# Storing a derived weight later, reading normalized rows back later, and choosing between operand and weights by what is scarce, in a fused graph layer

## The chip, the cores and the metric

The kernel runs on one core of a Trainium2 chip. The core has five engines that run side by side: TensorE (PE in the profile; its weight loads are PEld), VectorE (DVE), ScalarE (ACT), GpSimd (POOL) and SyncE (SP). Transfers are issued from queues of SP, ACT and POOL and run on 16 DMA engines. The metric is the device time of one execution in microseconds (us), as a median over several.

## The reference

Input are 32 graphs `b`, each with 512 nodes of 256 features, and an adjacency mask of 512 x 512 for each. All is computed in float32. Cut to what matters:

```python
h      = relu(layernorm(x))                      # [32, 512, 256]
c      = relu(bn(conv1(h)))                      # 1x1 convolution along the nodes
x_conv = relu(bn(conv2(c)) + h)                  # 17 taps, 256 -> 256 channels
s      = h @ w_se.T + b_se                       # 3 features
A      = exp(-|s_n - s_m|^2) * mask              # [512, 512] for each graph
x_nmp  = A @ relu(h @ w_msg.T + b_msg)
gi     = concat(x_conv, x_nmp) @ w_ih.T + b_ih   # GRU cell
gh     = h @ w_hh.T + b_hh
r, z   = sigmoid(gi_r + gh_r), sigmoid(gi_z + gh_z)
out    = x + (1 - z) * tanh(gi_n + r * gh_n) + z * h
```

## The kernel before

**Work.** Graphs come in 8 groups of 4. Five streams of work are interleaved by hand, each a Python generator:

- `rows` and `begins`: normalize a graph, turn it so that features lie on partitions, write that to DRAM (`HD`), and later run conv1 on it. For graphs 0 to 7 the turning is done by TensorE (`norm_t`); for graphs 8 to 31 it is done by the function `begin`: GpSimd's queue stores the normalized tile to DRAM (`XD_`, L791), SP's queue reads it back in 32-column blocks (8 transfers of 64 KB, `blocks`, L771), VectorE transposes the blocks in place (L799), GpSimd's queue stores the result (L802), and the input of the graph two further on is fetched.
- `conv`: the 17-tap convolution in a short-convolution form. For each group there are 25 products `m = 25 g + n`. Product `m` needs an operand `X2[m]`, which VectorE makes by subtractions from conv1's output, and a weight tile `WS[m]` in one of three buffers. In the first group (`m` below 25) VectorE and ScalarE make each weight from the 17 taps (`weights_first`), and ScalarE's queue stores it to DRAM. From `m = 25` on it is read back (`weights_again`, L470).
- In the second group (`m` from 25 to 49) a third part of each weight, the sum of its two parts, is made by VectorE in `third_weight` and stored by GpSimd's queue; from the third group on it is read back with the rest.
- `graphs`: messages, the factors of the squared distance (VectorE; `augl`, `augr`), their transposes, four exponentials (`kernel_exp`: four thin matmuls into `ps_b` and three `ps_g` banks, then four activations), the mask (`masked`; for graphs 0 to 7 TensorE transposes the mask tile `m_sb` and VectorE multiplies; for later graphs VectorE transposes), and the gather `A @ msg`. Mask tiles have three buffers; each use asks for the tile three further on.
- `gates`: the GRU matmuls into `ps_acc` and what follows them, from product 24 on. Before it `late_pools` (L686) loads the gates' weights (`whh` 768 KB, `wih` 1536 KB), and the first residual tiles (`res`, 8 transfers of 64 KB) follow on SP's queue.

**Order.** The scheduler is the loop at L1102. It keeps a planned clock `now`, which each matmul advances by an estimate, and planned times at which VectorE and ScalarE come free (`dve.free`, `act.free`). A generator yields the planned time at which it may go on. Work recorded with `later(t, f)` is issued when `now` reaches `t`. So a planned time does not make a queue wait; it sets where an instruction stands in the order of its queue. Each queue and engine then runs its instructions in that order and waits for semaphores. `background` fills VectorE with normalization, operands, weights and sums; its line L1013 asks first for an operand, then for a weight, then for a sum:

```python
near = at_product + 2
if len(X2) < near and operand_some() or len(WS) < near and prepare_some() or sum_some():
    return True
```

PSUM banks: `ps_c` has two, `ps_b` one, `ps_acc` two, `ps_g` three.

Of the kernel before, what the change touches and what calls it, by code (L numbers as in the profile page):

```python
# [44 lines left out]
def kernel(  # L45
# [28 lines left out]
    nc = tc.nc  # L74
# [23 lines left out]
    now = 5.0  # L98
# [23 lines left out]
    dve, act = Engine(nc.vector, 0.12, 0.00108), Engine(nc.scalar, 0.16, 0.0009)  # L122
# [21 lines left out]
    def later(t, f):  # L144
        LATER.append((t, f))
        LATER.sort(key=lambda e: e[0])
# [18 lines left out]
    def load(b, xs=None):  # L165
        if b not in XS:
            fetch(b, xs)
        NORMS[b] = norm(b)
        NORM_AT[b] = max(now + 7.0, 50.0) if b >= G else ARRIVES[b]
# [139 lines left out]
    def norm_t(b, d):  # L309
        xn = XS[b]  # L310
        if d == 0:
            HT[b] = front.tile([P, ND, N], F32, name="hT", bufs=2)
        ps = bank()
        for c in range(NT):
            turn(ps[:, c * P : (c + 1) * P], xn[:, c, d * P : (d + 1) * P])
        act.activation(HT[b][:, d, :], ps, AF.Relu)
        if d == ND - 1:
            XS.pop(b)
            nc.gpsimd.dma_start(HD[b], HT[b])
# [83 lines left out]
    WD = [dram.tile([P, 3, ND, D], F32, name=f"wd{n}") for n in range(25)]  # L403
# [17 lines left out]
    WS, W_AT = [], []  # L421
# [54 lines left out]
    def third_weight(m):  # L476
        if m in thirds:
            return
        thirds.add(m)
        w = WS[m]  # L480
        dve.tensor_tensor(w[:, 2], w[:, 0], w[:, 1], op=ALU.add)
        nc.gpsimd.dma_start(WD[m % 25][:, 2], w[:, 2])
        W_AT[m] = dve.free + LAG

    SUMS = []
# [96 lines left out]
    X2, X_AT, XD = [], [], {}  # L582
# [9 lines left out]
    def operand_some():  # L592

        nonlocal freed
        if len(X2) >= min(at_product + 1 + AHEAD, 25 * NG) or len(X2) >= 25 * made:
            return False
        if len(X2) == 25 * (made - 1) and now < made_at:
            return False
        got = next(xs)
        if got is not None:  # L600
            X2.append(got)
            X_AT.append(dve.free + LAG)
            if len(X2) % 25 == 21:
                freed = len(X2) // 25
        return True
# [3 lines left out]
    def prepare_some():  # L609
        nonlocal prepare_at  # L610
        if len(WS) >= 25 or len(WS) >= at_product + 3 or now < prepare_at:
            return False
        prepare_at = next(prepare)
        return True

    def convolution():
# [18 lines left out]
        for g in range(NG):  # L635
# [3 lines left out]
            for n in range(25):  # L639
# [8 lines left out]
                if 25 <= m + 1 < 50 and W_AT[m + 1] <= now:  # L648
                    third_weight(m + 1)
# [5 lines left out]
                if 25 <= m < 50:  # L655
                    third_weight(m)
                    yield W_AT[m]
# [110 lines left out]
    def blocks(t, rows, o):  # L768
        for g in range(P // 32):
            at = o * P + 32 * g  # L770
            nc.sync.dma_start(  # L771
                t[32 * g : 32 * g + 32, :].rearrange("i (k j) -> i k j", j=32),
                rows[:, :, at : at + 32],
            )
# [8 lines left out]
    def begin(b):  # L783

        nonlocal begun
        if b >= TURNED:
            yield lambda: b not in NORMS
            xs = XS.pop(b)  # L790
            nc.gpsimd.dma_start(XD_[b].rearrange("(c p) d -> p c d", p=P), xs)  # L791
            yield now + 4.5
            xb = xs.rearrange("p c d -> p (c d)").rearrange("p (o n) -> p o n", o=ND)
            for o in range(ND):
                blocks(xb[:, o, :], XD_[b].rearrange("(k i) d -> i k d", i=32), o)
            yield now + 8.0
            HT[b] = front.tile([P, ND, N], F32, name="hT", bufs=2)
            for o in range(ND):
                dve.transpose(HT[b][:, o, :], xb[:, o, :])  # L799
                if o < ND - 1:  # L800
                    yield dve.free
            nc.gpsimd.dma_start(HD[b], HT[b])  # L802
            begun = b + 1
            if b + 2 < B:
                load(b + 2)
            return
        if b == 2:
            yield lambda: told > 0
        yield lambda: b not in NORMS
        yield NORM_AT[b]  # L810
        for d in range(ND):
            norm_t(b, d)
            if d == ND - 1:
                begun = b + 1
                if b < 2 or b >= G:
                    load(b + (G if b < 2 else 2))
            yield now
# [177 lines left out]
    def sum_some():  # L995
        if not SUMS:
            return False
        SUMS.pop(0)()
        return True

    def norm_ahead(early=0.45):
        for b in list(NORMS)[:2]:
            if (b < G or clock["conv"] >= (b - G) / G - early) and norm_some(b):
                return True
        return False

    def background():

        nonlocal turn_of
        if norm_ahead(0.25):  # L1010
            return True
        near = at_product + 2
        if len(X2) < near and operand_some() or len(WS) < near and prepare_some() or sum_some():  # L1013
            return True
        for _ in range(3):
            turn_of += 1
            if (operand_some, norm_ahead, prepare_some)[turn_of % 3]():
                return True
        return False

    def fill():
        while LATER and LATER[0][0] <= now:
            LATER.pop(0)[1]()
        if EVAC:
            evacuate()
        while dve.free < now + 1.5 and background():
            pass
# [5 lines left out]
    def all_begins():  # L1033
        for b in range(G, B):
            yield lambda: b in XS and not rows_wait
            yield from begin(b)
# [3 lines left out]
    def all_rows():  # L1040
        nonlocal rows_wait
        for b in range(B):
            if b < G:
                yield from begin(b)
                yield act.free + LAG
            else:
                yield lambda: freed >= b // G - 1 and begun > b
                rows_wait = True
                load_row(b)
                yield now + 8.0  # L1050
            yield from rows(b)
            rows_wait = False
# [121 lines left out]
```

## Time and profile before

| | us |
|---|---|
| median of 4 runs | 2154.92 (2154.06 to 2155.49) |
| the profiled execution | 2154.06 |
| its span, first to last instruction | 2152.3 |
| TensorE busy in the span | 2095.5 (97%) |
| VectorE busy | 1523.1 (71%) |
| ScalarE busy | 762.1 (35%) |
| DMA read and written | 282.74 MB and 82.58 MB |

The span is what the engines' instructions cover; some 1.8 us of the execution lie around it. A busy share is an average over stages: the first 165 us make the weights of the first group, around 205 to 235 us the gates' weights are loaded, the last 150 us have only gates. Where TensorE is busy nearly all the time, what counts is when it is idle, on what it then waits, and at which clock it runs: PEclk is the granted share of the full clock, and a stage at 0.5 takes twice as long for the same matmuls. A wait is put down to the instruction whose semaphore came last.

### The profile page before, as it was taken

What the parts mean: (1) busy time and instruction counts of PE and PEld (TensorE: products, weight loads), DVE (VectorE), ACT (ScalarE), POOL (GpSimd) and SP (SyncE); (2) the same over time, 40 slices, a digit from 0 to 9 for tenths busy, and PEclk for the clock granted to TensorE, in tenths of its full rate; (3) what the DMA queues carried; (4) which work ended last, traced back from release to release, by engine and by line L of the source; (5) the groups of instructions that cost most, each with busy time, mean ns of one, the idle gap of its engine ahead of it and who ended that gap; (6) DMA issues with size and microseconds to landing.
All of it is one profiled execution on the core that took longest, in us unless ns stands there. A gap on an engine that the chain in (4) does not pass through costs nothing.

```text
span 2152.3 us, 26543 instructions
## 1 busy us (share of the span) xinstructions
PE 2095.5 (97%) x9200; PEld 1299.2 (60%) x9200; DVE 1523.1 (71%) x2818; ACT 762.1 (35%) x1277; POOL 296.2 (14%) x445
## 2 busy tenths in 40 slices
PE   7999799999999999999999999999999999999998
PEld 4877575566665666656665666656666566665443
DVE  6896788677776777667885777767777677776333
ACT  5545332433233342234324153243522324222311
POOL 2100112111111111111111111110111010011111
PEclk9999899999999999999999999999999999999999
DMA  7436667757676667765776766756675565554331
GB/s 271 171 133 224 207 208 199 203 158 192 150 225 163 176 177 200 201 191 144 204 189 183 207 151 187 196 168 189 180 193 150 152 162 144 148 160 92 69 74 35
DMA packets 539462, 367.12 MB, mean 171 GB/s; under 512 B 455232, under 2 KB 472000, under 8 KB 538688
## 3 DMA queue, kind: packets, MB, share of 16 engines
q1 hardware_dynamic: 511392, 282.95, 48.9%
q0 software_dynamic: 23248, 69.23, 10.1%
q10 hardware_dynamic: 4688, 13.24, 1.6%
q8 instruction: 73, 1.20, 0.2%
q14 instruction: 61, 0.50, 0.1%
HBM read 282.74 MB, written 82.58 MB: 170 GB/s over the span
## 4 chain that ended last, share of the span: by engine, by line
PE 95%; DVE 2%; ACT 1%; SPq 1%; DMA 0%; issue 0%; POOL 0%; ACTq 0%; DVEq 0%; POOLq 0%
PE ps_acc L127 46%; PE ps_g L127 20%; PE ps_c L127 19%; PE ps_b L127 7%; PE ps_g L132 2%; PE ps_b L733 1%; SPq L771 1%; ACT at L118 0%; ACT xconv L118 0%; DMA m_sb<-in_adj_dram 0%; DVE xconv L118 0%; DVE x L118 0%; PE ps_g L733 0%; ACT x_sb L118 0%; DMA x_sb<-in_x_dram 0%
## 5 line engine op out<-in xcount | busy, mean ns | idle before, releaser
L127 PE MATMUL ps_acc<-xconv,wih 128*128 128x512 f32 (+1 forms) x772 | 362.8, 592 | 6.0 <-ACT xconv L118 5.9
L127 PE MATMUL ps_acc<-xnb,wih 128*128 128x512 f32 (+1 forms) x772 | 362.6, 592 | 0.0
L127 PE MATMUL ps_acc<-hTb,whh 128*128 128x512 f32 x768 | 357.3, 595 | 0.0
L127 PE MATMUL ps_c<-xd,w 128*128 128x116 f32 x2800 | 343.0, 276 | 0.0
L127 PEld LDWEIGHTS ps_c<-xd,w 128*128 128x128 f32 x2800 | 329.3, 193 | 3.3 <-issue 3.1
L922 POOL DMA_DIRECT2D out_dram<-res x252 | 164.7, 660 | 976.4 <-DVE res L118 873.1
L118 DVE TENSOR_TENSOR r<-ps_acc,r 128x512 f32<-128x512 f32 (+1 forms) x65 | 44.4, 684 | 315.8 <-PE ps_acc L127 315.8
L127 PEld LDWEIGHTS ps_acc<-xnb,wih 128*128 128x128 f32 x772 | 141.6, 189 | 162.3 <-issue 160.4
L127 PEld LDWEIGHTS ps_acc<-xconv,wih 128*128 128x128 f32 x772 | 141.7, 190 | 159.6 <-issue 147.3
L127 PEld LDWEIGHTS ps_acc<-hTb,whh 128*128 128x128 f32 x768 | 142.1, 191 | 149.4 <-issue 145.4
L127 PE MATMUL ps_g<-at,msg 128*128 128x512 f32 x512 | 226.7, 593 | 0.9 <-DVE at L118 0.9
L127 PEld LDWEIGHTS ps_b<-x,w 128*128 128x128 f32 x1400 | 183.1, 192 | 69.8 <-issue 54.9
L118 ACT ACTIVATE mid<-ps_b 128x232 f32<-128x232 f32 x175 | 63.9, 365 | 369.3 <-PE ps_b L127 333.4
L127 PE MATMUL ps_b<-x,w 128*128 128x116 f32 x1400 | 184.6, 275 | 4.7 <-ACT at L118 4.7
L127 PEld LDWEIGHTS ps_g<-at,msg 128*128 128x128 f32 x512 | 96.1, 190 | 115.9 <-issue 111.4
L118 DVE SCALAR_TENSOR_TENSOR x<-x,x 128x480 f32<-128x480 f32 (+1 forms) x184 | 143.9, 782 | 2.8
L118 DVE TENSOR_TENSOR x<-x 128x240 f32<-128x240 f32 (+1 forms) x320 | 135.2, 462 | 0.6
L127 PE MATMUL ps_g<-wmsg,hTg 128*128 128x259 f32 x496 | 124.7, 382 | 0.7 <-ACT hT L118 0.7
L127 PE MATMUL ps_g<-hT,w 128*128 128x512 f32 x256 | 120.1, 613 | 2.3 <-ACT at L118 2.3
L127 PEld LDWEIGHTS ps_g<-wmsg,hTg 128*128 128x128 f32 x496 | 92.5, 190 | 45.1 <-issue 33.5
L118 DVE TENSOR_TENSOR xd<-x 128x480 f32<-128x480 f32 x175 | 113.5, 649 | 8.7 <-PE ps_c L127 8.7
L118 ACT ACTIVATE z<-ps_acc,brz 128x512 f32<-128x512 f32 x64 | 44.0, 687 | 208.6 <-PE ps_acc L127 208.4
(109 smaller groups left out, 2485.0 us busy)
## 6 DMA issues: line engine op xcount, KB each, us to landing
w<-wd SPq DMA_DIRECT2D x150, 768.0 KB, 5.9
m_sb<-in_adj_dram SPq DMA_DIRECT2D x384, 64.0 KB, 2.6
hd<-hT POOLq DMA_DIRECT2D x32, 512.0 KB, 6.0
res<-in_x_dram SPq DMA_DIRECT2D x256, 64.0 KB, 4.3
hTb<-hd SPq DMA_DIRECT2D x32, 512.0 KB, 6.2
xnb<-nd SPq DMA_DIRECT2D x64, 256.0 KB, 3.2
out_dram<-res POOLq DMA_DIRECT2D x252, 64.0 KB, 3.2
hTg<-hd SPq DMA_DIRECT2D x31, 512.0 KB, 4.4
```

Source lines behind the costliest of these rows:

```text
L118: getattr(self.engine, name)(*tiles, **more)
L127: nc.tensor.matmul(ps, lhsT, rhs, **more)
L132: nc.tensor.transpose(ps, a, ident)
L733: nc.tensor.matmul(pss[c], gr.left[k, :], gr.right[k, :], start=True, stop=True, tile_position=(32 * c, 0),)
L771: nc.sync.dma_start(t[32 * g : 32 * g + 32, :].rearrange("i (k j) -> i k j", j=32), rows[:, :, at : at + 32],)
L922: queue.dma_start(OB[b][:, s.start // 32 : s.stop // 32, o * P + 32 * g : o * P + 32 * g + 32], y[at, s].rearrange("i (k j) -> i k j", j=32),)
```

## The change

Three edits. In `third_weight` the store of the third part is recorded with `later` at VectorE's planned end plus 0.4, instead of at once; it stays on GpSimd's queue and there are 25 of it. In `begin` the planned time between the store of the normalized tile and its reading back goes from 4.5 to 7.0, for graphs 8 to 31. In `background` the two lists are sorted by length, and the shorter one is served first; at equal length the weights come first, where the operand did. All three alter where instructions stand in the queues; none adds or removes an instruction.

```diff
@@ third_weight
         dve.tensor_tensor(w[:, 2], w[:, 0], w[:, 1], op=ALU.add)
-        nc.gpsimd.dma_start(WD[m % 25][:, 2], w[:, 2])
+        later(dve.free + 0.4, lambda: nc.gpsimd.dma_start(WD[m % 25][:, 2], w[:, 2]))
         W_AT[m] = dve.free + LAG
@@ begin
             nc.gpsimd.dma_start(XD_[b].rearrange("(c p) d -> p c d", p=P), xs)
-            yield now + 4.5
+            yield now + 7.0
             xb = xs.rearrange("p c d -> p (c d)").rearrange("p (o n) -> p o n", o=ND)
@@ background
         near = at_product + 2
-        if len(X2) < near and operand_some() or len(WS) < near and prepare_some() or sum_some():
+        first = [(len(WS), prepare_some), (len(X2), operand_some)]
+        for n, some in sorted(first, key=lambda e: e[0]):
+            if n < near and some():
+                return True
+        if sum_some():
             return True
```

## The prediction

> **What bounds the kernel now.** I read the totals of the page first, then TensorE's waits, then busy time and clock by stretch, then SP's queue where the longest wait lies.
>
> ```profile
> span 2152.3 us, 26543 instructions
> PE 2095.5 (97%) x9200; PEld 1299.2 (60%) x9200; DVE 1523.1 (71%) x2818; ACT 762.1 (35%) x1277; POOL 296.2 (14%) x445
> ```
>
> TensorE is the bound. The changed program has the same matmuls in another order, so time can only come from its 57 us of idleness and from stretches at a lower clock. Its waits, over the whole span (who waits, for whom, total us, times, longest):
>
> ```profile
> PE ps_g L132 <- DMA m_sb<-in_adj_dram: 13.1, 1, 13.1
> PE ps_g L132 <- ACT x_sb L118: 9.3, 1, 9.3
> PE ps_acc L127 <- ACT xconv L118: 5.9, 5, 1.4
> PE ps_b L127 <- ACT at L118: 4.7, 5, 1.6
> PE ps_c L127 <- ACT w L118: 3.5, 2, 3.2
> PE ps_g L132 <- DVE augl L118: 2.4, 1, 2.4
> ```
>
> The 9.3 is the start and 5.2 of the xconv row lie in the last 150 us; both keep their order. The rest is within reach: one wait for a mask tile at 215.6 us, and many small ones between 60 and 150 us. Busy time by stretch (us, then PE, PEld, DVE, ACT, POOL with counts, then PEclk, DMA share, GB/s):
>
> ```profile
> 100.00:165.00 65.00, 59.73 (x417) 52.64 (x416) 57.09 (x101) 27.10 (x51) 4.30 (x5) 0.90 0.45 163
> 133.50:140.70 7.20, 3.49 (x17) 2.31 (x21) 7.03 (x17) 2.61 (x5) 0.54 (x1) 0.98 0.62 222
> 140.70:150.90 10.20, 8.69 (x43) 7.18 (x35) 8.11 (x21) 5.95 (x11) 1.31 (x1) 0.51 0.48 180
> 219.20:232.80 13.60, 4.11 (x8) 2.26 (x9) 8.07 (x15) 8.18 (x8) 1.10 (x2) 0.51 0.90 204
> 235.00:350.00 115.00, 114.28 (x590) 77.41 (x589) 95.25 (x190) 38.86 (x65) 22.61 (x35) 1.00 0.67 209
> 350.00:2000.00 1650.00, 1643.85 (x7119) 1007.30 (x7118) 1201.96 (x2190) 572.44 (x947) 223.90 (x329) 1.00 0.64 174
> ```
>
> The dearest lull apart from the mask is 133.5 to 150.9: TensorE idle for 3.71 + 1.51 us, then at half clock, which costs 8.69 x 0.49 = 4.3; together 9.5. VectorE is 88% busy from 100 to 165, so it is the next bound there. From 235 to 2000 TensorE loses under 7 us. SP's queue around the mask wait (start, us):
>
> ```profile
> 203.67 1.72 SPq L470 DMA_DIRECT2D w<-wd  x2
> 205.49 0.37 SPq L692 DMA_DIRECT2D whh<-in_w_hh_dram  x1
> 205.91 0.53 SPq L693 DMA_DIRECT2D wih<-in_w_ih_dram  x1
> 206.54 0.55 SPq L470 DMA_DIRECT2D w<-wd  x1
> 207.15 13.88 SPq L771 DMA_DIRECT2D res<-in_x_dram  x8
> 222.60 1.47 SPq L262 DMA_DIRECT2D m_sb<-in_adj_dram  x2
> ```
>
> The mask stands behind the gates' weights and eight `res` pieces: 24.9 us pass from the first `w` here to its landing (228.6), while TensorE arrives after 11.9.
>
> **The change, part by part.** Numbers are us, minus is faster. "New order" is the order in which the changed program's instructions stand on each engine and queue; durations are from the rows before.
>
> Edit 3, first effect, at 62 to 66 us: the fourth weight. TensorE waits 3.17 for ScalarE's `w`. Before, four `x_sb` activations (2.06) run ahead of it, in the new order two, so it comes 1.0 earlier. The half-clock stretch behind it (65.6 to 69.0) stays. A: **-1.0**, between -3.2 (whole wait) and 0 (the input for `w` is late too).
>
> Edit 3, second effect, graph 2's exponentials (134 to 151). Before, VectorE has two 1536-wide weight additions (1.75 + 1.76) between the second and third message; now there is one 1440-wide operand step (1.65). In front of the first message the new order has 0.8 more. So `augl` comes about 1.1 to 2.1 earlier, and 0.3 to 1.3 of the 2.38 wait is left; I take 0.9. The wait of 0.69 for `right` stays. The next two (1.14 for the exponentials, 0.38 for `w`) go: a whole product (32 records, 3.56) now stands between exponentials and mask, with its weight made before. Left are 1.6 idle and one half-clock stretch like that at 65.6 (3.4 x 0.47 = 1.6), 3.2 in place of 9.5. B: **-6.3**, between -9.5 and 0.
>
> What is late next is VectorE. In the new order graph 1's last mask is followed by its gather with no product between, so the multiplication (0.68) and what is queued before it is exposed; and two operands of the later products are made only shortly before TensorE comes to them, since it comes earlier. VectorE has 65 - 57.09 = 7.9 idle from 100 to 165, and 12.9 of 40 from 165 to 205, so most of A and B can be kept, not all. C: **+2.0**, between 0 (its idle time covers it) and +6.3 (all of B given back).
>
> The loading stage (203 to 233). Before, `hT` of graph 7 is ahead of the gates' weights on SP, which stood there until 203.26 (5.8 of it put down to a store). In the new order it is behind them, so loading can start when product 23 ends, 4.8 of TensorE's work earlier; the mask is needed 3.5 earlier. The mask still stands behind `w`, `whh`, `wih`, `w`, `res`, `hTb`, two `xnb`, and now that `hT` (512 KB); a store of `xd` (512 KB) leaves the stretch in exchange. From product 23's end TensorE has 2 x 1.78 of product, 1.1 of exponentials, 3.45 of conv1, 1.3 of transposes and a 1.15 wait for `at` until that mask: 10.6, against 11.9 before, so the wait itself grows by about 1.3 while its start comes 1.3 sooner. After the mask the gather now follows at once and waits for VectorE's multiplication, about 1.0, where gate matmuls stood; but one extra stop of SP is gone. D: **0**, between -15 (13.1 and the half clock behind it, 4.11 x 0.49) and +7.3 (one more block like the longest `res` issue).
>
> Exponentials followed directly by a product in `ps_b`, which has one bank: before this happens five times after 600 us, and each is a wait in the fourth row of the waits (0.67 to 1.62, mean 0.93; two are followed by 3.3 at clock 0.53, 1.55 lost each). By the new order there are six: two new (graph 4, and one near 1610 us), one gone (near 1300). E: **+1.5** = 0.93 + 3.1 / 5, between 0 and +3.2.
>
> Edit 1: 25 stores of 0.55 on GpSimd's queue. Before, 16 of them waited there, 110.5 in total, with `nd`, `xd`, `hd` and `out` stores behind; now these go first. The reload of a third part comes 25 products later, over 100 us, and the next weight load into the same buffer waits for a store that lands in 3.6. No TensorE wait hangs on either: **0**; if the cover goes, the five waits of weight loads on such stores (15.2 on SP) are the size, 0 to +3.
>
> Edit 2: 24 readbacks, each 8 issues (4.3 to 6.6 on SP), moved 2.5 later and thereby behind one or two weight, mask, `res` or fetch issues. SP waits 108.2 in 15 of them; at most 15 x 2.5 of it goes. What hides it: after 235 us TensorE has no wait on a DMA at all. VectorE's transposes, the `hd` store and the fetch of the graph two further on move too; conv1 needs them a group later. **0**, between -1.5 (a half-clock stretch less) and +3 (two more like 1427 us, 1.6 each).
>
> Sum: -1.0 - 6.3 + 2.0 + 0 + 1.5 = **-3.8**. Against the profiled execution's 2154.06 that is 2150.3; the median shown is 0.86 higher, so 2151.1.
>
> One rule bears on B and E. Rows first: 1.04 idle at 736.2 is followed by a stretch at 0.53; waits of 0.67 are not. The Trainium skill, page "TensorE: Matmul & The Clock Gate", section "HAM oscillation", asks only that TensorE have no idle gap over about 3.4 us. By that, waits of 1 to 3 us cost themselves alone; B would be -3.6, E +0.9, and the sum -1.7 (2153.2). The rows decide, and short waits are dearer than the rule says.
>
> **Rivals.** (1) The mask wait shrinks. For it: loading starts earlier by TensorE's work, and `xd` competes less. Against: as many bytes stand ahead of the mask, DMA share 0.9 to 1. With half of 13.1 and of the 2.0 of half clock behind it gone: 2151.1 - 7.6 = 2143.5. (2) Gains and new waits cancel, since VectorE sets the pace up to 205: C takes all of A and B, leaving E and its like: 2155 to 2157. (3) Slower: VectorE falls behind and each of three places where TensorE now waits for an operand or a mask product costs 2 to 3 and sets off a half-clock stretch of 1.6: 3 x (2.5 + 1.6) + 1.5 - 7.3 = +6.5, so 2161. It decides once those waits exceed about 1 us, the size that set off the clock before. For it: 88% busy. Against: 7.9 idle there. That the change does little of what it says is part of (2): SP's waits for `xd` are mostly longer than 2.5.
>
> **How the numbers follow.** My sum 0.42 (own range 2147 to 2154), rival 1 0.16, rival 2 0.14, rival 3 0.28. A measurement tells about 0.2% (4.3 us) from no change, so the line is at 2150.6: half of my case and rival 1 are faster (0.38), the other half and most of rival 2 within (0.32), the rest slower (0.30). The range 2140 to 2165 leaves out a fully vanished mask wait and more than rival 3.
>
> **What would show it.** A: the `w` wait near 62 us about 2. B: no stretch at half clock of 10 us near 140, `augl` wait under 1.3. C: new waits of `ps_c` or `ps_g` on DVE before 205, in sum near 2; over 5 speaks for rivals 2 or 3. D: one `m_sb` wait of 11 to 15; under 7 is rival 1. E: six `ps_b` waits. Edits 1 and 2: no TensorE wait on a DMA after 240; SP's `xd` wait under 108.2. I am wrong if a wait on a DMA appears after 240, or if the clock shows many more low stretches before 205.

## The result, and the profile after

The changed kernel takes 2160.54 us (median of 31 executions, 2157.54 to 2164.78), the kernel before 2155.26 (51 executions, 2152.12 to 2160.19). The ratio is 1.0022, with a 95% interval of 1.0017 to 1.0027: it is slower, by 5.3 us. The forecast was 2151.1, a gain. The time lies inside the stated range and where rival 3 put it (2161), but neither at the places that rival 3 named nor for its reason.

The profiled execution of the changed kernel took 2162.24, 1.7 above its median; that of the kernel before 2154.06, 1.2 below its own. So the two traces differ by 8.2, the medians by 5.3. The totals of the page after:

```profile
span 2160.1 us, 26532 instructions
PE 2096.2 (97%) x9200; PEld 1300.4 (60%) x9200; DVE 1523.5 (71%) x2818; ACT 763.6 (35%) x1277; POOL 296.8 (14%) x445
```

TensorE's busy time is the same within 0.7, its idle time went from 56.8 (2152.3 - 2095.5) to 63.9. So 7.1 of the 7.8 us that the span grew by is waiting; the mean granted clock is 0.989 in both profiles, since new stretches at half clock after 235 us replace longer ones before. TensorE's waits after (who waits, for whom, total us, times, longest):

```profile
PE ps_g L132 <- DMA m_sb<-in_adj_dram: 14.5, 1, 14.5
...
PE ps_b L127 <- ACT at L118: 5.3, 6, 1.6
PE ps_acc L127 <- ACT xconv L118: 5.2, 4, 1.3
PE ps_c L127 <- DVE z L118: 4.3, 2, 2.2
PE ps_c L127 <- DVE x L118: 2.7, 1, 2.7
PE ps_g L127 <- DVE at L118: 2.5, 3, 0.9
PE ps_c L127 <- ACT w L118: 2.2, 1, 2.2
PE ps_c L127 <- DVE sq L118: 1.9, 1, 1.9
PE ps_g L132 <- DVE augl L118: 1.2, 1, 1.2
```

Against before, `w` lost 1.3, `augl` 1.2, and three waits on ScalarE some 2.7 together. New are `z` (4.3, two waits), `x` (2.7) and `sq` (1.9), all of `ps_c` on VectorE; `m_sb` grew by 1.4, `at` on VectorE by 1.6, the `ps_b` row by 0.6. Busy time by stretch (us, then PE, PEld, DVE, ACT, POOL with counts, then PEclk, DMA share, GB/s):

```profile
235.00:350.00 115.00, 110.07 (x555) 75.91 (x554) 94.03 (x182) 40.11 (x65) 19.60 (x31) 0.97 0.62 184
350.00:2000.00 1650.00, 1643.82 (x7136) 1008.62 (x7135) 1203.97 (x2205) 571.09 (x949) 226.01 (x332) 1.00 0.64 176
```

The row to look at is 235 to 350. Before, TensorE was busy for 114.28 of it at a clock of 1.00; now for 110.07 at 0.97. From 350 to 2000 the two agree within 0.03. So the loss lies where the prediction had reckoned with next to none (under 7 us from 235 to 2000, in the order of before).

The SP queue around the mask, after, is the counterpart of the queue that the prediction shows of before. The weights, the eight residual pieces and the mask behind them are still in that order, and the mask tiles are asked at 216.65, while TensorE had been waiting since 208.6:

```profile
200.14 0.42 SPq L692 DMA_DIRECT2D whh<-in_w_hh_dram  x1
200.61 0.51 SPq L693 DMA_DIRECT2D wih<-in_w_ih_dram  x1
203.12 0.33 SPq L470 DMA_DIRECT2D w<-wd  x1
203.50 11.10 SPq L771 DMA_DIRECT2D res<-in_x_dram  x8
...
216.65 7.89 SPq L262 DMA_DIRECT2D m_sb<-in_adj_dram  x4
```

**The two new waits.** TensorE from 292 to 301 us (start, duration, engine, line, operation, count, and in brackets the idle time before it and its releaser):

```profile
292.01 1.04 PE L127 MATMUL ps_b<-x,w 128*128 128x116 f32 x8
292.89 1.95 PE L127 MATMUL ps_c<-xd,w 128*128 128x116 f32 x16
294.68 1.06 PE L127 MATMUL ps_b<-x,w 128*128 128x116 f32 x8
297.94 3.31 PE L127 MATMUL ps_c<-xd,w 128*128 128x116 f32 x16 [2.20 <-DVE z L118]
```

Two products follow each other. The second one's `ps_c` needs a bank that VectorE has not emptied yet. ScalarE and VectorE meanwhile:

```profile
290.50 0.60 ACT L118 ACTIVATE at<-ps_g 128x512 f32<-128x512 f32 x1 [2.84 <-PE ps_g L127]
292.21 0.69 ACT L118 ACTIVATE r<-ps_acc,brz 128x512 f32<-128x512 f32 x1 [1.12 <-PE ps_acc L127]
293.10 0.36 ACT L118 ACTIVATE mid<-ps_b 128x232 f32<-128x232 f32 x1 [0.19 <-PE ps_b L127]
293.36 3.86 ACT L118 ACTIVATE y<-z 128x1392 f32<-128x1392 f32 x3
...
297.25 0.64 DVE L118 TENSOR_TENSOR z<-ps_c,mid 128x464 f32<-128x464 f32 x1 [6.15 <-ACT y L118]
```

VectorE is idle for 6.15 us. It is to write the next `z`, which has one buffer, and ScalarE still has to read the old `z` three times (`y<-z`). The old `z` was complete at 288.9; the copies stand in ScalarE's queue behind three steps that wait for TensorE, so they start at 293.36. The kernel before has the same three copies at 277.25, where no product runs from 273.5 to 284.5:

```profile
277.25 3.86 ACT L118 ACTIVATE y<-z 128x1392 f32<-128x1392 f32 x3
```

Each fifth product starts a new `z`; here that place fell on two products in a row.

The second wait, at 332.60, is also for `z`, which starts at 331.92 there, and has another reason: `sum_all` (L487), which runs before a new `z`, ends with `settle`, which issues everything that was recorded for later. There that was the end of graph 0's gates:

```profile
326.86 1.61 DVE L118 TENSOR_TENSOR y<-y,z 128x1392 f32<-128x1392 f32 x1
328.39 0.68 DVE L118 TENSOR_TENSOR o_sb<-hTb,r 128x512 f32<-128x512 f32 x1
...
331.31 0.69 DVE L118 TENSOR_TENSOR res<-o_sb,res 128x512 f32<-128x512 f32 x1
331.92 1.18 DVE L118 TENSOR_TENSOR z<-ps_c,mid 128x464 f32<-128x464 f32 x2
...
332.60 3.66 PE L127 MATMUL ps_c<-xd,w 128*128 128x116 f32 x16 [2.06 <-DVE z L118]
```

Behind the first wait 16 matmuls take 3.31, behind the second 3.66, where 1.95 is usual: a stretch at half clock follows each (granted clock 0.58 from 297.9 to 301.3, 0.54 from 332.6 to 336.3). Together that is 2.20 + 1.36 + 2.06 + 1.71 = 7.3. The first stretch runs on into the next four matmuls (1.47 at 301.04, where 1.05 is usual), some 0.4 more.

### The profile page after: what moved, and what is told of

Read it like the earlier page. It is cut to its first block, busy times and chain, and to the rows that moved or that the text cites. A ratio compares the mean times of both kernels' runs of the same rounds, so it can differ in the third digit from the quotient of the medians.

```text
span 2160.1 us, 26532 instructions
## 1 busy us (share of the span) xinstructions
PE 2096.2 (97%) x9200; PEld 1300.4 (60%) x9200; DVE 1523.5 (71%) x2818; ACT 763.6 (35%) x1277; POOL 296.8 (14%) x445
## 4 chain that ended last, share of the span: by engine, by line
PE 83%; ACT 1%; DVE 1%; issue 0%; DVEq 0%; ACTq 0%
PE ps_acc L127 44%; PE ps_g L127 17%; PE ps_c L127 14%; PE ps_b L127 7%; PE ps_b L733 1%; PE ps_g L132 1%; ACT at L118 0%; DVE xconv L118 0%; ACT xconv L118 0%; ACT L118 0%; DVE r L118 0%; DVE o_sb L118 0%; PE ps_g L733 0%; DVE msg L118 0%; DVE res L118 0%
## 5 line engine op out<-in xcount | busy, mean ns | idle before, releaser
L118 ACT ACTIVATE mid<-ps_b 128x232 f32<-128x232 f32 x175 | 63.9, 365 | 370.7 <-PE ps_b L127 335.1
```

Source lines behind the costliest of these rows:

```text
L118: getattr(self.engine, name)(*tiles, **more)
```

## The experiments

**Each edit alone, and 2 with 3.** The theory after the first look was that the two waits are the loss, and that edit 2 had brought them. The rivals were that edit 3 leaves VectorE behind, and that it takes both.

```diff
+ edit3_only: before, with the sorted lists in background
+ edit2_only: before, with yield now + 7.0 in begin
+ edits_2_and_3: after, with the store of the third weight issued at once
```

> Before with edit 3 alone (scarcer of operand and weights made next). Theory 1 (the loss of the changed kernel is the pair of waits of TensorE on VectorE near 298 and 333 us and the half-clock stretch behind each, and edit 2 put the work into that order): those two waits are absent here, the early gains stay and are given back by 231 us, so 2153 to 2157. Theory 2 (edit 3 alone leaves VectorE behind when the gates begin, edit 2 does nothing): the two waits are here, 2159 to 2162. Theory 3 (both needed): the early part as in the changed kernel, 235 to 350 us without a wait over 1 us.

> Before with edit 2 alone (readback 7.0 instead of 4.5 after the store). TensorE's order is that of before except for places after some 280 us. Theory 1: waits of ps_c or ps_g on VectorE of about 2 appear between 280 and 350 us, 2157 to 2161. Theory 2: none appear, 2153 to 2157. If SP's wait for xd falls under before's 108.2 by up to 15 x 2.5 = 37 and the time does not move, that wait was worth nothing.

> The changed kernel without edit 1: the third weights are stored at once again. Edit 1 costed at 0 (0 to +3): 2160.5 within 1.5, and the two waits near 298 and 333 us are still there. If edit 1 matters, 2157 to 2159 or under.

Measured: edit 3 alone 2153.55 (ratio to before 0.9993, 0.9985 to 1.0002); edit 2 alone 2154.63 (0.9996, 0.9987 to 1.0005); edits 2 and 3 together 2161.28 (1.0023, 1.0014 to 1.0031). Neither edit shows a loss alone; the two together are the whole loss. Edit 1 has no measurable worth, as 2161.28 without it and 2160.54 with it show. TensorE's waits after 240 us with edit 3 alone hold no `z`; these are the three largest (the second in the last 150 us):

```profile
PE ps_b L127 <- ACT at L118: 5.4, 6, 1.6
PE ps_acc L127 <- ACT xconv L118: 5.2, 4, 1.3
PE ps_g L127 <- ACT at L118: 1.2, 1, 1.2
```

With edit 2 alone TensorE is busy for 114.27 of the 115 us from 235 to 350, as before. SP's wait for `xd` fell from 108.2 to 64.8 with edit 2 alone. The time didn't move with it beyond its interval, so that wait was worth nothing that shows. Theory 1 and theory 2 fall; theory 3 stands. That theory 3 is a matter of order can be read in the programs and the traces: edit 3 has no direct effect after product 24, since from then on weights are only read back; but it hands over another planned state, in which the 2.5 us of edit 2 move other instructions than they do in the kernel before. With edit 2 alone TensorE's matmuls stand in the order of before up to 854 us, past both places; with edits 2 and 3 they leave the order of edit 3 alone at 253 us.

The profile of edit 3 alone is of its slowest execution (2157.73): its 235 to 350 us also have a clock of 0.97, because a stretch at half clock follows two short waits (0.69 and 0.77) near 319. The comparison therefore rests on the medians and on the waits, not on that one time.

**How many of the 24 readbacks matter.**

```diff
-            yield now + 7.0
+            yield now + (7.0 if b == 9 else 4.5)     readback_of_graph_9
+            yield now + (4.5 if b < 10 else 7.0)     readback_from_graph_10
```

> The changed kernel with the later readback (7.0) for graph 9 alone; graphs 8 and 10 to 31 keep 4.5. TensorE's order is then the changed kernel's up to about 315 us. Theory A (one moved readback shifts the plan so that products come back to back where VectorE moves on to the next z; the other 23 cost nothing): the wait of about 2.2 for z near 298 us with its half-clock stretch is there, the one at 333 perhaps not, 2155 to 2160. Theory B (all 24 readbacks cost a little by later landing): no wait near 298, 2153.5 to 2154.5.

> The changed kernel with 4.5 for graphs 8 and 9 and 7.0 from graph 10 on. TensorE's order is that of edit 3 alone up to about 330 us. Theory A: no wait of ps_c on z between 285 and 350 us, 2152 to 2156. Theory B: 2159 to 2161.

Measured: 2158.38 (1.0014, 1.0005 to 1.0023) with graph 9's readback alone, 2154.83 (0.9998, 0.9989 to 1.0007) with graphs 10 to 31. One moved readback out of 24 brings the first wait, and 22 of them show no cost. Which readback the second wait needs besides was not isolated. With graph 9 alone the wait stands one instruction earlier, since the three copies are ahead of `mid` in ScalarE's queue and `ps_b` has one bank; its size is the same:

```profile
296.68 1.15 PE L127 MATMUL ps_b<-x,w 128*128 128x116 f32 x8 [2.12 <-ACT mid L118]
297.67 3.17 PE L127 MATMUL ps_c<-xd,w 128*128 128x116 f32 x16
```

The place at 333 has no wait there, as theory A allowed; one of 0.93 for VectorE's `w` stands at 321.9. Theory B falls.

**Each wait's cause by itself.** These kernels keep the changed kernel's order of TensorE and the scheduler's charges.

```diff
@@ copies_split: summed, copy
+                if g != 1 or scale == 1.0:
                     act.activation(dst, src, AF.Copy, scale=scale)
+                    return
+                act.free = max(act.free, now) + act.fixed + act.each * elements(src)
+                nc.vector.tensor_scalar(dst, src, scale, None, op0=ALU.mult)
@@ thin_gate_end: mix_last and leave, graph 0, second half
+            thin = slice(0, 32) if (b, o) == (0, 1) else s
...
+                nc.vector.tensor_tensor(d[:, thin], p[:, thin], q[:, thin], op=op)
```

> The changed kernel with its order kept; of the three copies y<-z at the start of conv2's second group (3.86 on ScalarE, issued behind steps that wait for TensorE) two run on VectorE, which was idle for 6.15 there, the plan charged as before. If z near 297 us is late because those copies still read it: the wait of 2.20 at 298 and its half-clock stretch (1.4) go, the one at 333 stays, 2160.5 - 3.6 = 2157. If the copies are not what z waits for: the wait stays, 2160.5.

> The changed kernel with its order kept, but the five VectorE steps that end graph 0's gates in the second half of its columns (three of o_sb and r, the transposition, res) work on 32 of 512 elements, so part of one output block is not the reference's; the plan is charged as before. They are about 3.4 us of VectorE's queue right ahead of z near 332 us. If z is late because those steps were issued ahead of it: the wait of 2.06 at 332.6 and its half-clock stretch (1.7) go, the one at 298 stays, 2160.5 - 3.8 = 2156.7. If z is late for another reason: still 2.06, 2160.5.

> Both together: the two copies on VectorE, and the end of graph 0's gates in its second half on 32 of 512 elements (part of one output block is then not the reference's). If the two waits near 298 and 333 us are the whole loss of the changed kernel, no wait of ps_c is left between 235 and 350 us and the time is that of edit 3 alone, 2153 to 2154.5. If something else costs too: over 2156.

With the copies split, 2158.35 (1.0015, 1.0006 to 1.0023). The first wait is gone, the second still 2.06. VectorE makes its two copies while it would have been idle, and the next `z` starts 3.3 earlier:

```profile
292.58 1.36 ACT L118 ACTIVATE y<-z 128x1392 f32<-128x1392 f32 x1
...
290.24 3.10 DVE L507 TENSOR_SCALAR y<-z 128x1392 f32<-128x1392 f32 x2
293.97 0.64 DVE L118 TENSOR_TENSOR z<-ps_c,mid 128x464 f32<-128x464 f32 x1 [0.63 <-ACT y L118]
...
294.81 1.95 PE L127 MATMUL ps_c<-xd,w 128*128 128x116 f32 x16
```

With the gate's end thin, 2157.70 (1.0007, 0.9998 to 1.0016). The first wait is still 2.20; the second is gone, and its product runs at full clock:

```profile
328.05 0.18 DVE L908 TENSOR_TENSOR o_sb<-hTb,r 128x32 f32<-128x32 f32 x1
...
329.08 1.18 DVE L118 TENSOR_TENSOR z<-ps_c,mid 128x464 f32<-128x464 f32 x2
...
330.05 1.95 PE L127 MATMUL ps_c<-xd,w 128*128 128x116 f32 x16
```

With both, 2152.84 (0.9990, 0.9981 to 0.9999): not above edit 3 alone (2153.55), and no wait on VectorE or ScalarE over 0.7 between 235 and 350 us. The stretch is back at what before had:

```profile
235.00:350.00 115.00, 114.33 (x591) 77.66 (x590) 102.10 (x202) 38.50 (x63) 21.40 (x34) 1.00 0.66 197
```

The thin end leaves work out. Whether the same steps, issued behind the new `z`, would do as well was not tried.

So the two waits with their clock stretches are the whole loss of the changed kernel, and the cause of each is shown: old `z` still being read by copies that stand behind steps waiting for TensorE, and a gate's end issued ahead of the new `z`. One by one they gave 2.2 and 2.8, together 7.7; the intervals of each (about 1.9 us to either side) allow some of that difference, and I don't explain the rest.

**The mask wait, which both kernels have.** It was the dearest single wait and the prediction's term D, so I moved what stands ahead of it on SP's queue: first everything, then the residual pieces alone, then these and the gates' weights.

```diff
@@ before_late_loads: whh and wih leave late_pools; in all_gates
         yield lambda: late is not None
+        yield now + 12
+        nc.sync.dma_start(whh, w_hh)
+        nc.sync.dma_start(wih, w_ih)
+        yield now + 0.5
         for o in range(ND):
             load_res(0, o)
@@ before_late_res (on before), edit3_late_res (on edit3_only): no load_res in all_gates; in gates
             yield from products(ps_r, o, 0, 1, 3, (0, 2), reset)
+            if b == 0 and o == 0:
+                load_res(0, 0)
+                load_res(0, 1)
@@ edit3_mask_first: edit3_late_res, and whh and wih in all_gates behind yield now + 10
```

> Before, with the loads of the gates' weights (whh, wih), of the first residuals, hidden states and sums issued 12 planned us later, so that on SP's queue two or three of the four mask tiles stand ahead of 2.3 MB and of the eight residual pieces. If the mask wait of 13.1 at 215 us is only that queue: it falls to under 4 and the half clock behind it (2.0) goes too, so 2155.3 - 9 - 2 = 2144, unless the gates' first products then wait for whh (the row to look at), which would give back up to all of it: 2144 to 2155. If the mask is late for another reason, m_sb still waits over 10.

Measured: 2160.06 (1.0016, 1.0007 to 1.0025), slower than before and above the 2144 to 2155 that I expected. The mask wait is gone, and TensorE waits longer for the gates' hidden states, which now stand behind the weights and the residual pieces, and 4.1 once for VectorE's `at`:

```profile
PE ps_acc L127 <- DMA hTb<-hd: 16.0, 1, 16.0
```

The wait had only changed its name. In the kernel before, a gate product comes right behind the mask.

> Before, without any of the three edits, with the residual pieces late. If the gain of the run with edit 3 is the queue alone: mask wait 13.1 down by 5 to 8, 2147 to 2150. If edit 3's order (gather and conv1 right after the mask, the gates' first product 16 us later instead of at once) is what lets the gain be kept: the first gate product waits for whh, wih or hTb instead, 2152 to 2155.

> Before with edit 3 alone, and the eight residual pieces of graph 0 asked after its first gate's products instead of right behind the gates' weights. On SP they took 11.3 of the 16.6 between the weights and the mask. If the mask wait (14.7) is that queue: the mask is asked at about 206 and lands after the 4.25 MB ahead of it at some 400 GB/s, near 212, wait 3 to 5, and part of the half clock behind it goes: 2153.5 - 10 - 2 = 2141 to 2144. If the bytes are the limit and not the queue, the wait stays over 10: 2150 to 2154. A new wait of the gates on res would show as a wait of VectorE near 275.

Measured: 2148.77 on before (0.9968, 0.9955 to 0.9980) and 2148.73 with edit 3 (0.9971, 0.9959 to 0.9982). The gain, 6.5 and 4.8, does not need edit 3's order: without and with it the mask wait falls to 9.3 and 9.0, and no gate waits for its weights. Without edit 3:

```profile
PE ps_g L132 <- DMA m_sb<-in_adj_dram: 9.3, 1, 9.3
```

With edit 3 I had expected a wait of 3 to 5 and 2141 to 2144, or over 10 if the bytes are the limit; it is neither. Moving the pieces takes their eight issues and their 0.5 MB out of the stretch at once, so queue and bytes are not told apart here. The mask tiles of that run are now asked at 206.05, but their four issues take 11.95 us on SP, of which 3.3 are put down to the landing of `wih` and 5.5 to an earlier mask tile.

> Before with edit 3, the residual pieces late as in the run before (2148.7 there, mask wait 9.0), and the two loads of the gates' weights asked 10 planned us later, so that all four mask tiles stand ahead of them. In the order of edit 3 the gates' first product comes some 16 us after the mask, enough for 3.25 MB at 400 GB/s (8). Expected: mask wait 2 to 4, no new wait on whh, wih or hTb, 2148.7 - 6 = 2142 to 2144. If the gates then wait for their weights: 2146 to 2150.

Measured: 2144.37 (0.9954, 0.9940 to 0.9967), the fastest, 10.9 below before and 16.2 below the changed kernel, just above the 2142 to 2144 expected. The four mask tiles go ahead of the 2.3 MB, their issues take 5.96, and no wait for a mask is left:

```profile
206.03 5.96 SPq L262 DMA_DIRECT2D m_sb<-in_adj_dram  x4
212.08 0.38 SPq L1061 DMA_DIRECT2D whh<-in_w_hh_dram  x1
...
210.51 1.12 PE L132 MATMUL ps_g<-ident,m_sb 128*128 128x128 f32 x4 [2.94 <-DVE at L118]
213.83 6.56 PE L127 MATMUL ps_g<-at,msg 128*128 128x512 f32 x8 [2.19 <-DVE at L118]
```

What is late next is VectorE's mask multiplication, 2.94 and 2.19. The gates don't wait for `whh`, `wih` or `hTb`. Edit 3's order leaves the gathers, conv1 and the next graph's messages between the mask and the first gate product. Whether the kernel before could take the weights as late, with the residual pieces out of the way, was not tried.

## Why the prediction was wrong

**A, right.** The wait for `w` is 2.18 (forecast about 2).

**B, right for the waits, unsafe for the clock.** `augl` waits 1.20 (forecast 0.9), the 1.14 and 0.38 are gone, and there is no stretch of 10 us at half clock near 140. But the 10.2 us at half clock of the one profile that the term started from were not the order's own: three later runs with the same order of TensorE (edit 2 alone, `before_late_loads`, `before_late_res`) show 6.8 there, and seven of the ten profiles with edit 3 show 6.8 as well, near 137. So the part of B that came from the clock (2.7) is not a safe gain.

**C, mis-sized.** It stood at 2.0. In the changed kernel's profile the new waits on VectorE before 205 are 2.73 (`ps_c` at 154.6), 1.91 (`ps_c` at 190.5) and 0.78 (`ps_g` at 116.0), 5.4 in sum. By the prediction's own sign that is over the mark (5) for rivals 2 and 3. In other executions of the same order the 2.73 was 0.5 or less, and the sum 3.5 in that with the gate's end thin (0.34 + 1.91 + 1.20): there the half-clock stretch came earlier, at 137 to 138, TensorE was slower, and the product behind the wait started only about 1 us earlier. So what comes earlier in this stretch is in part waited for again, and A and B could only be kept in part.

**D, right in kind.** One `m_sb` wait of 14.5, inside 11 to 15, and 0.78 for the gather; 1.4 + 0.8 against the 0 that I took. The 1.4 is less than executions differ by: in the order of before the same wait was 13.1 in one profile and 17.6 in another (edit 2 alone).

**E, right.** Six `ps_b` waits on `at`, 0.6 more in sum where 1.5 was forecast.

Taken together these five are edit 3 alone, for which the sum said -3.8; measured -2.05 against the 2155.60 of before in that comparison (interval -3.2 to +0.4). The interval holds 0 and leaves out -3.8: a gain is not shown, and the size was too large. C, and the clock's part of B, are the terms that were off; how much each cost is not separated.

**Edit 1, right:** no measurable effect.

**Edit 2, the step that failed.** Its working was "What hides it: after 235 us TensorE has no wait on a DMA at all", and that is still true: after 240 TensorE has none, and SP's wait for `xd` is 88.6, under 108.2. Edit 2 alone is worth 0, as forecast. What failed is that the step priced the readback as transfers which land later, and added it to the other edits. A later planned time doesn't only move the transfer. The scheduler goes on issuing until then, and VectorE's transposes, its sums and the products behind them take other places. With edit 3 in place the new order has two places where a new `z` falls on products without room around them, 7.3 us in the profiled execution. Both places stand in the changed program's order, which the prediction used for its other terms, and the sum had no term for them: it looked for VectorE's new waits before 205 alone and took "From 235 to 2000 TensorE loses under 7 us" from the order of before, which no longer held.

**Rivals.** Rival 3 had the size of the waits (2 to 3, with a stretch of 1.6 behind each) and the time, 2161. That the time fits is luck: it meant three places before 205 and a VectorE with too much to do, while the two waits that made the loss lie after 235, and at the first of them VectorE itself stood idle for 6.15. Rival 1 didn't happen: in the eight profiles with edit 3 and SP's loads unmoved the mask wait is 14.0 to 15.6. Rival 2 (2155 to 2157) is not excluded for edit 3 alone, whose interval reaches 2156.

**The rule on the clock.** The waits here were 2.20, 2.06 and 2.12, and 16 matmuls behind them took 3.31, 3.66 and 3.17 where 1.95 is usual. The Trainium skill, page "TensorE: Matmul & The Clock Gate", section "HAM oscillation — how this bites in real kernels", asks for no idle gap of TensorE over about 3.4 us. The measurement decides: without the stretches the two waits of the changed kernel would have cost 4.3 instead of 7.3.

## What to carry to other kernels

Where a scheduler lays out the queues, a changed planned time is a changed order. Price it from the listing of the new order over the whole span, not from the transfer that it names, and don't add edits that share one scheduler: two that showed no loss alone cost about 5 us here together. Look first at the points where a buffer without a spare is reused, since what stands ahead of the reuse in each queue decides whether TensorE gets through. The wait behind the full queue of loads moved here to the next load when its own was put first; it went only when what was not yet needed left that stretch.

## What the runs showed of the hardware that was not expected

The same waits at the same place were followed by a half-clock stretch in one execution and not in another. Behind the waits for `augl` and `right` (1.20 and 0.69) the next 32 matmuls took 3.83 in the changed kernel's profile and 6.40 in that of the thin gate's end, whose order is the same up to there. Behind 1.91 for `sq` 16 matmuls took 2.01 in the one and 3.37 in the other. Even short waits can do it: 0.69 and 0.77 near 319 in the profile of edit 3 alone were followed by 16 matmuls in 3.62, though the prediction had read from waits of 0.67 that such do nothing.

The traces show one thing more. In each of the 14 profiles all changes of the granted clock, from the first recorded one on, lie on one grid of steps of 3.41 us, so a low stretch lasts 3.4 us or a multiple, save one that the end cuts off. Where the grid stands against the program differs between executions. These are the two steps at the waits for `augl` and `right`, first in the changed kernel, then with the thin gate's end (window, us, then busy times with counts, then PEclk, DMA share, GB/s):

```profile
134.63:138.05 3.42, 1.83 (x10) 1.09 (x8) 2.81 (x10) 1.75 (x4) 0.00 (x0) 1.00 0.88 334
138.05:141.46 3.41, 3.12 (x26) 2.36 (x27) 3.32 (x8) 2.20 (x6) 0.00 (x0) 1.00 0.66 268
...
133.78:137.20 3.42, 1.53 (x11) 0.87 (x13) 2.94 (x10) 1.50 (x3) 0.00 (x0) 1.00 1.03 388
137.20:140.61 3.41, 3.41 (x17) 2.02 (x10) 3.31 (x10) 1.95 (x5) 0.00 (x0) 0.50 0.50 203
```

The same waits are cut by the grid in another way, and TensorE is busy for 1.83 of the first step in one and 1.53 in the other. That this decides is not shown: in the profile of edit 3 alone a step with 2.36 busy (315.82 to 319.24) is followed by a low one too.

So executions of one program differ by several us (2157.5 to 2164.8 for the changed kernel), and a single profile can't tell two orders apart when they differ by 3.
